# Second layer of a two-layer convolution kernel: three shared scale-and-result buffers, output stores on two queues, a split addition, shifted quantised rows

## The chip, the cores and the metric

The kernel runs on one core of a Trainium2 chip (trn2). The metric is the device time of one execution in microseconds. The profile is one further execution, recorded by the hardware profiler; its times count from the start of its span.

## The reference

The input x is 32 images of 8 channels, 256 x 256, float32. Two layers follow each other, each added to its own input:

```python
x = x + layer0(group_norm(x))     # a coupled map lattice of 15 steps, two small networks, a gate
x = x + layer1(group_norm(x))     # a quantised 3x3 convolution, 8 channels to 8
```

The change touches layer 1 alone. It quantises its normalised input with one scale for the whole batch, convolves whole numbers, scales back and adds a bias:

```python
def layer1(x, weight, bias):
    sx = 127 / max(abs(x));  sw = 127 / max(abs(weight))
    qx = clip(round(x * sx), -127, 127);  qw = clip(round(weight * sw), -127, 127)
    return conv3x3(qx, qw, padding=1) / (sx * sw) + bias
```

## The kernel before, in words

The first layer takes most of the time. Its program (lattice, hidden network, gate) works on groups of four images and leaves in a scratch tensor of device memory, `y_s[b]`, the sum x + layer0 of each image, with the image's mean, inverse deviation and largest deviation in small tiles. The maximum over the batch is needed before anything can be quantised, so the second layer starts only when the first is complete.

The second layer is the block `with ExitStack() as two` (from L879). An image is held as a tile of 128 partitions x 19 x 256 floats (`NB` = 19 bands, 2432 KB). A partition is one of 16 image rows of one of 8 channels; bands start 14 rows apart, so 14 of the 16 rows of a band are results and the outer two are the neighbours that a 3x3 convolution needs. Per image b, in the order of the source:

- the loads: three images ahead, one DMA of the whole tile `yb` (four buffers, pool `yp`). The first three are issued by SP, the others by ACT, after the activations of image b (L890, called at L936 to L937);
- L921: the scaling, three VectorE (DVE) instructions (first band, the 17 middle bands, last band) from `yb` into `tq`, the only buffer of its pool;
- L925: the rounding in place, by adding and taking away a large constant;
- L927: the clipping, written as bf16 into `qt`, one of two tiles taken in turn, whose rows are 258 wide: a zero at column 0, 256 values from column 1, a zero at column 257;
- L934: ten groups (two bands each, the last one band) of three TensorE (PE) matmuls, one for each horizontal shift dx, which read `qt` from column dx. Each group has one of four PSUM buffers `pt2`;
- L935: for each group a ScalarE (ACT) activation, which scales, adds the bias and writes two bands of `ob`, the result (two buffers, pool `op`);
- L938: one DVE addition of the whole tile, `ob` + `yb`;
- L941: 19 stores, one per band, each 14 rows of 8 channels (112 KB; the last band 4 rows, 32 KB), all issued by SP.

The order on each engine is the order of the source as the framework's scheduler moves it; it also puts in the waits. A buffer is given to its next user when all who read it are done, and a store is a reader of `ob`. Completion of a DMA is told by a semaphore; the program has eight of them for the DMAs of SP and ACT together and hands them out in turn, in the order in which it lists the DMAs. A DMA is issued only when the DMA that had its semaphore before has landed.

In the program as built the loads stand in pairs: the load of b+3 and that of b+4 lie one after the other on ACT's list, behind the activations of image b+1, and the second also waits for a buffer of `yb`. DVE's list takes the quantising of an image ahead of the addition of the image before.

Of the kernel before, what the change touches and what calls it, by code (L numbers as in the profile page):

```python
# [31 lines left out]
F32 = mybir.dt.float32  # L32
BF16 = mybir.dt.bfloat16
F32R = mybir.dt.float32r
AF = mybir.ActivationFunctionType
ALU = mybir.AluOpType
# [4 lines left out]
P = 128  # L41
C = 8
H = W = 256
# [3 lines left out]
MAX_Q = 127.0  # L47
ROUND = 1.5 * 2.0**23

NB = 19  # L50
STEP = 14
PW = W + 2
# [61 lines left out]
def kernel(  # L114
# [15 lines left out]
    nc = tc.nc  # L130
    B = x.shape[0]
    V, S, G, T = nc.vector, nc.scalar, nc.gpsimd, nc.tensor

    def dram_ap(t, offset, dims):
        return bass.AP(t.tensor, t.offset + offset, dims)
# [17 lines left out]
    qw = cp.tile([P, 3, P], BF16, name="qw")  # L153
# [103 lines left out]
    with ExitStack() as one:  # L257

        one.enter_context(tc.manual_schedule(engines={mybir.EngineType.PE}))
        pool = lambda name, bufs, **kw: one.enter_context(tc.tile_pool(name=name, bufs=bufs, **kw))  # L260
# [558 lines left out]
        def chain(*gens):  # L819
            for gen in gens:  # L820
                yield from gen
# [15 lines left out]
        def both(a, t_a, b, t_b):  # L837

            done_a = done_b = 0.0
            while a or b:  # L840
                if b is None or a and done_a * t_b <= done_b * t_a:
                    w = next(a, None)
                    if w is None:
                        a = None
                        continue
                    done_a += w
                else:
                    w = next(b, None)
                    if w is None:
                        b = None  # L850
                        continue
                    done_b += w
                yield w

        def prep(g, halves):
            return normalise([(b, half) for half in halves for b in range(g * GB, g * GB + GB)])

        def images(f, g):
            for b in range(g * GB, g * GB + GB):
                yield from f(b)  # L860
# [5 lines left out]
        for g in range(NG):  # L866
            fill, t = images(nca, g), T_NCA
            if g:
                fill, t = both(fill, t, images(gate, g - 1), T_GATE), t + T_GATE
            if g + 1 < NG:  # L870
                fill, t = both(fill, t, prep(g + 1, (0, 1)), T_PREP), t + T_PREP
            if g == 0:
                fill, t = chain(prep(0, (1,)), fill), t + 20.0
# [5 lines left out]
    with ExitStack() as two:  # L879


        pool = lambda name, bufs, **kw: two.enter_context(
            tc.tile_pool(name=name, bufs=bufs, reuse_waits="tile", **kw)
        )
        tp, qp, op, sp, yp = pool("tp", 1), pool("qp", 2), pool("op", 2), pool("sp", 1), pool("yp", 4)
        ps = pool("ps", 4, space=PSUM)

        def load(b):
            y = yp.tile([P, NB, W], F32, name="yb", tag="yb")
            (nc.sync if b < 3 else nc.scalar).dma_start(  # L890
                y, dram_ap(y_s[b], 0, [[W, P], [STEP * C * W, NB], [1, W]])
            )
            return y

        ys = {b: load(b) for b in range(3)}

        gmax = sp.tile([P, 1], F32, name="gmax")
        V.tensor_reduce(gmax, dev_y, AX.X, ALU.max)
        gall = sp.tile([P, 1], F32, name="gall")
        G.partition_all_reduce(gall, gmax, P, bass.bass_isa.ReduceOp.max)  # L900
        sx = sp.tile([P, 1], F32, name="sx")
        V.reciprocal(sx, gall)
        V.tensor_scalar(sx, sx, MAX_Q, None, ALU.mult)
        inv = sp.tile([P, 1], F32, name="inv")
        V.tensor_tensor(inv, sx, sw, ALU.mult)
        V.reciprocal(inv, inv)
        qs = sp.tile([P, 3, B], F32, name="qs")
        V.tensor_scalar(qs[:, 0, :], rstd_y, sx, None, ALU.mult)
        V.tensor_scalar(qs[:, 1, :], qs[:, 0, :], masks[:, 2:3], None, ALU.mult)
        V.tensor_scalar(qs[:, 2, :], qs[:, 0, :], masks[:, 3:4], None, ALU.mult)  # L910
        qt = [qp.tile([P, NB, PW], BF16, name=f"qt{i}", tag=f"qt{i}", bufs=1) for i in range(2)]
        for t in qt:
            V.memset(t[:, :, 0], 0.0)
            V.memset(t[:, :, PW - 1], 0.0)

        for b in range(B):
            y = ys.pop(b)

            t = tp.tile([P, NB, W], F32, name="tq", tag="tq")
            for k0, k1, i in ((0, 1, 1), (1, NB - 1, 0), (NB - 1, NB, 2)):  # L920
                V.tensor_scalar(  # L921
                    t[:, k0:k1, :], y[:, k0:k1, :], mean_y[:, b : b + 1], qs[:, i, b : b + 1],
                    ALU.subtract, ALU.mult,
                )
            V.tensor_scalar(t, t, ROUND, ROUND, ALU.add, ALU.subtract)  # L925
            q = qt[b % 2]
            V.tensor_scalar(q[:, :, 1 : 1 + W], t, MAX_Q, -MAX_Q, ALU.min, ALU.max)  # L927
            o = op.tile([P, NB, W], F32, name="ob", tag="ob")
            for p in range(10):
                k0, n = 2 * p, (2 if p < 9 else 1)  # L930
                pt = ps.tile([P, 512], F32, name="pt2", tag="pt2")
                pt = pt[:, : n * W].rearrange("p (k w) -> p k w", w=W)
                for dx in range(3):
                    T.matmul(pt, qw[:, dx, :], q[:, k0 : k0 + n, dx : dx + W], start=(dx == 0), stop=(dx == 2))  # L934
                S.activation(o[:, k0 : k0 + n, :], pt, AF.Identity, bias=bv[:, 3:4], scale=inv)  # L935
            if b + 3 < B:  # L936
                ys[b + 3] = load(b + 3)  # L937
            V.tensor_tensor(o, o, y, ALU.add)  # L938
            for k in range(NB):
                rows = STEP if k < NB - 1 else 4  # L940
                nc.sync.dma_start(  # L941
                    dram_ap(out, b * C * H * W + STEP * k * W, [[W, rows], [H * W, C], [1, W]]),
                    o[C : C + rows * C, k, :],
                )


# [43 lines left out]
```

## Time and profile before

| what | us |
|---|---|
| median of three runs | 14468.11 (14463.03 to 14472.73) |
| the profiled execution | 14447.83 |
| its span | 14446.0 |
| PE busy over the span | 13241.2 (92%) |
| DVE busy | 8161.7 (56%) |
| ACT busy | 4043.5 (28%) |
| POOL busy | 2458.8 (17%) |
| in the stretch 13680 to 14446: PE / DVE / ACT busy | 269.16 / 520.88 / 219.13 |
| in the same stretch: share of time the DMA engines are busy, mean rate | 0.61, 187 GB/s |

The page gives busy times for the whole program, and there the first layer dominates. The second layer is the last stretch: its first scaling starts at 13682.90 us and its last store is issued at 14442.98. Rows by line, waits and timelines can be asked for that stretch alone. In the views, a chain of waits lists the work that ended last, followed back from the end: at each step to what released it. "issue" is time in which nothing that the profile shows was waited for; SPq and ACTq are the issuing of DMAs by those engines; a row "DMA yb<-y_s" is the time from the issue of a load until it has landed.

### The profile page before, as it was taken

To read this page: it belongs to the slowest core of one execution; us is meant where nothing else is said; L and a number is where in the kernel's file an instruction comes from. 1 tells how busy PE (TensorE), PEld (TensorE's weight loads), DVE (VectorE), ACT (ScalarE), POOL (GpSimd) and SP (SyncE) were. 2 spreads that over 40 slices of the span, in tenths; PEclk is the share of its full clock that TensorE was granted. 3 is DMA by queue.
4 is the path that set the end of the run, shared out by engine and by line. 5 is a ranking of instruction groups with operands and counts; after the bars stand their busy time and mean duration, and the time that the engine had idled before them with its cause. 6 is when DMAs were issued, how large, how long until landed. Compare 5 with 4: busy or idle time off the path is not lost.

```text
span 14446.0 us, 229162 instructions
## 1 busy us (share of the span) xinstructions
PE 13241.2 (92%) x81728; PEld 6420.6 (44%) x81728; DVE 8161.7 (56%) x16290; ACT 4043.5 (28%) x6274; POOL 2458.8 (17%) x4266
## 2 busy tenths in 40 slices
PE   2999999999999999999999999999999999999733
PEld 1554444444444444444444444444444444444211
DVE  3555555555555555555555555555555555555576
ACT  1333223232322232222223222322232222222122
POOL 1110111111111111111111111111111111112300
PEclk9999999999999999999999999999999999999866
DMA  5444444444444444444344434444444433333365
GB/s 149 93 101 93 92 99 105 101 95 104 105 97 101 106 98 98 101 100 111 88 101 105 108 91 102 103 108 94 97 104 108 95 84 80 86 75 79 114 195 176
DMA packets 2259557, 1496.71 MB, mean 104 GB/s; under 512 B 1061248, under 2 KB 2229504, under 8 KB 2258304
## 3 DMA queue, kind: packets, MB, share of 16 engines
q1 hardware_dynamic: 2176976, 1401.95, 41.1%
q10 hardware_dynamic: 81456, 80.12, 1.7%
q8 instruction: 663, 10.86, 0.3%
q14 instruction: 462, 3.78, 0.1%
HBM read 866.48 MB, written 478.69 MB: 93 GB/s over the span
## 4 chain that ended last, share of the span: by engine, by line
PE 76%; DVE 7%; DMA 7%; SPq 4%; issue 3%; ACT 1%; POOL 1%; ACTq 1%; POOLq 0%; DVEq 0%
PE pt L486 34%; PE ph L563 19%; PE pa L755 13%; PE acc L580 7%; DVE gt L494 2%; PE pg L721 1%; DMA im<-xp_s 1%; DMA out_dram<-ob 1%; SPq L941 1%; PE pt L934 1%; DVE m_b L499 1%; DMA yb<-y_s 1%; DMA m_a<-m_a 1%; DMA xb<-in_x_dram 1%; DMA xr<-in_x_dram 1%
## 5 line engine op out<-in xcount | busy, mean ns | idle before, releaser
L486 PE MATMUL pt<-m_a,lw 128*64 128x390 f32 x17280 | 5857.6, 497 | 160.4 <-DMA m_a<-m_a 121.4
L486 PE MATMUL pt<-m_b,lw 128*64 128x384 f32 x17280 | 5825.7, 492 | 23.0 <-DVE m_b L410 17.8
L573 ACT ACTIVATE h<-ph,bp_sb 128x512 f32<-128x512 f32 x4096 | 2584.7, 685 | 6258.0 <-PE ph L563 6187.8
L486 PEld LDWEIGHTS pt<-m_a,lw 128*64 128x64 f32 x17280 | 2312.1, 138 | 1824.9 <-issue 1670.8
L486 PEld LDWEIGHTS pt<-m_b,lw 128*64 128x64 f32 x17280 | 2316.1, 138 | 1601.4 <-issue 1465.6
L563 PE MATMUL ph<-im,wp_hi 48*128 48x512 f32 x12288 | 2713.5, 416 | 104.8 <-DMA im<-xp_s 54.4
L494 DVE SCALAR_TENSOR_TENSOR gt<-pt,d_b 128x390 f32<-128x390 f32 x2880 | 1610.6, 559 | 1828.2 <-PE pt L486 1824.9
L494 DVE SCALAR_TENSOR_TENSOR gt<-pt,d_a 128x384 f32<-128x384 f32 x2880 | 1584.9, 550 | 1826.9 <-PE pt L486 1826.5
L563 PE MATMUL ph<-im,wp_lo 48*128 48x512 f32 x12288 | 2598.5, 399 | 0.0
L503 POOL TENSOR_TENSOR m_b<-m_b,junk 128x12 f32<-128x12 f32 x2688 | 809.2, 301 | 8089.7 <-DVE m_b L499 7597.8
L563 PEld LDWEIGHTS ph<-im,wp_hi 48*128 48x128 f32 x12288 | 1331.4, 188 | 1013.5 <-DVE m_b L499 197.8
L499 DVE SCALAR_TENSOR_TENSOR m_b<-gt 128x390 f32<-128x390 f32 x2688 | 1562.5, 581 | 42.5 <-DVE gt L494 0.9
L499 DVE SCALAR_TENSOR_TENSOR m_a<-gt 128x384 f32<-128x384 f32 x2688 | 1525.9, 568 | 15.6
L563 PEld LDWEIGHTS ph<-im,wp_lo 48*128 48x128 f32 x12288 | 1327.1, 188 | 215.2
L580 PE MATMUL acc<-h,wu_z 128*32 128x512 f32 x8320 | 1170.7, 605 | 12.9 <-ACT h L573 7.3
L755 PE MATMUL pa<-xnb,gw 128*64 128x512 f32 (+1 forms) x3840 | 890.5, 596 | 0.2
L755 PE MATMUL pa<-cmb,gw 128*64 128x512 f32 (+1 forms) x3840 | 852.0, 576 | 10.0 <-POOL cmb L677 10.0
L755 PE MATMUL pa<-nb,gw 128*64 128x512 f32 (+1 forms) x3840 | 849.5, 574 | 0.0
L726 POOL TENSOR_TENSOR d<-cmb,nb 128x512 f32<-128x512 f32 x320 | 511.4, 1598 | 1608.5 <-DVE gate L730 1449.6
L730 DVE TENSOR_TENSOR gate<-gate,d 128x512 f32<-128x512 f32 x320 | 216.0, 675 | 870.3 <-ACT gate L723 856.3
L934 PE MATMUL pt<-qt,qw 128*128 128x512 bf16 (+1 forms) x960 | 269.2, 451 | 477.9 <-ACT ob L935 427.1
L767 ACT ACTIVATE r<-pa,bv 128x512 f32<-128x512 f32 x320 | 213.1, 666 | 1651.3 <-PE pa L755 1650.3
(132 smaller groups left out, 6966.1 us busy)
## 6 DMA issues: line engine op xcount, KB each, us to landing
im<-xp_s SPq DMA_DIRECT2D x1152, 193.5 KB
im<-xp_s SPq DMA_DIRECT2D x1216, 96.8 KB
d_a<-xq_s SPq DMA_DIRECT2D x2048, 36.0 KB
nb<-nc_s SPq DMA_DIRECT2D x288, 256.0 KB
cq<-cm_s SPq DMA_DIRECT2D x288, 256.0 KB
yb<-y_s ACTq DMA_DIRECT2D x29, 2432.0 KB
xb<-in_x_dram SPq DMA_DIRECT2D x544, 128.0 KB
xp_s<-hi SPq DMA_DIRECT2D x256, 258.0 KB
```

The source lines that it names most:

```text
L486: T.matmul(pt[half], lw[:, c, k, half], beside if part == 2 else own, start=part < 2, stop=part > 0,)
L494: V.scalar_tensor_tensor(gt, pt, FLOOR, d[:, ts, :], ALU.max, ALU.add)
L499: V.scalar_tensor_tensor(to, gt, 1.0, gt, ALU.subtract, ALU.mult)
L503: G.tensor_tensor(edge, edge, junk.unsqueeze(1).to_broadcast([P, 6, 2]), ALU.mult)
L563: T.matmul(ph[:, :n].rearrange("p (h w) -> p h w", w=W), w[64 * i : 64 * i + 48, dx, :], rhs[:, :, dx : dx + W], start=(dx == 0 and w is w ...
L573: S.activation(h[:, :n], ph[:, :n], AF.Relu, bias=bp_sb)
L580: T.matmul(acc[32 * g : 32 * g + 32, :cols], wu_z[:, 24 - 8 * i : 56 - 8 * i], h, start=first, stop=last,)
L726: G.tensor_tensor(three(d), cmb[:, :n, 1 : 1 + W], nin, ALU.subtract)
L730: V.tensor_tensor(y[:, :cols], gt[:, :cols], d[:, :cols], ALU.mult)
L755: T.matmul(three[half], gw[:, s * 3 + dx, half], t[:, :n, dx : dx + W], start=(i == 0), stop=(i == 8),)
L767: S.activation(r1[:, : n * W], pa[:, : n * W], AF.Relu, bias=bv[:, 0:1])
L934: T.matmul(pt, qw[:, dx, :], q[:, k0 : k0 + n, dx : dx + W], start=(dx == 0), stop=(dx == 2))
```

## The change

The scaled input and the result now share a buffer: `t` and `o` are one tile of the pool `op`, which has three buffers in place of two, and the pool `tp` is gone. An activation writes over values that the clipping has read. The rows of `qt` are 260 wide, with two zeros on each side and the 256 values from column 2; the matmuls read from columns 1, 2 and 3. The addition is made in two instructions, bands 0 to 9 and bands 10 to 18. The stores of bands 0 to 9 are issued by SP after the addition; those of bands 10 to 18 are issued by ACT one image later, after the next image's activations and the next load, and the last image's after the loop.

```diff
-        tp, qp, op, sp, yp = pool("tp", 1), pool("qp", 2), pool("op", 2), pool("sp", 1), pool("yp", 4)
+        qp, op, sp, yp = pool("qp", 1), pool("op", 3), pool("sp", 1), pool("yp", 4)
...
-        qt = [qp.tile([P, NB, PW], BF16, name=f"qt{i}", tag=f"qt{i}", bufs=1) for i in range(2)]
+        qt = [qp.tile([P, NB, W + 4], BF16, name=f"qt{i}", tag=f"qt{i}") for i in range(2)]
         for t in qt:
-            V.memset(t[:, :, 0], 0.0)
-            V.memset(t[:, :, PW - 1], 0.0)
+            V.memset(t[:, :, 0:2], 0.0)
+            V.memset(t[:, :, W + 2 : W + 4], 0.0)
+
+        def store(queue, b, o, ks):
+            for k in ks:
+                rows = STEP if k < NB - 1 else 4
+                queue.dma_start(
+                    dram_ap(out, b * C * H * W + STEP * k * W, [[W, rows], [H * W, C], [1, W]]),
+                    o[C : C + rows * C, k, :],
+                )
+
+        waiting = None
         for b in range(B):
             y = ys.pop(b)
-            t = tp.tile([P, NB, W], F32, name="tq", tag="tq")
+            t = op.tile([P, NB, W], F32, name="ob", tag="ob")
...
-            V.tensor_scalar(q[:, :, 1 : 1 + W], t, MAX_Q, -MAX_Q, ALU.min, ALU.max)
-            o = op.tile([P, NB, W], F32, name="ob", tag="ob")
+            V.tensor_scalar(q[:, :, 2 : 2 + W], t, MAX_Q, -MAX_Q, ALU.min, ALU.max)
+            o = t
...
-                    T.matmul(pt, qw[:, dx, :], q[:, k0 : k0 + n, dx : dx + W], start=(dx == 0), stop=(dx == 2))
+                    T.matmul(pt, qw[:, dx, :], q[:, k0 : k0 + n, dx + 1 : dx + 1 + W], start=(dx == 0), stop=(dx == 2))
                 S.activation(o[:, k0 : k0 + n, :], pt, AF.Identity, bias=bv[:, 3:4], scale=inv)
             if b + 3 < B:
                 ys[b + 3] = load(b + 3)
-            V.tensor_tensor(o, o, y, ALU.add)
-            for k in range(NB):
-                rows = STEP if k < NB - 1 else 4
-                nc.sync.dma_start(
-                    dram_ap(out, b * C * H * W + STEP * k * W, [[W, rows], [H * W, C], [1, W]]),
-                    o[C : C + rows * C, k, :],
-                )
+            if waiting:
+                store(nc.scalar, *waiting)
+            for ks in (slice(0, 10), slice(10, NB)):
+                V.tensor_tensor(o[:, ks, :], o[:, ks, :], y[:, ks, :], ALU.add)
+            store(nc.sync, b, o, range(0, 10))
+            waiting = (b, o, range(10, NB))
+        store(nc.scalar, *waiting)
```

In the changed program as built, from image 3 on, each image has the same list. ACT: ten activations of image b, the load of b+3, nine stores of b-1. SP: ten stores of b. DVE: the first two scalings of b+1, the two additions of b, the last scaling, the rounding and the clipping of b+1. The scaling of b+1 waits for all stores of b-2, whose buffer it writes.

## The prediction

> **What bounds the kernel now.** I looked first at the page's slices: TensorE is full until the last three of 40, so only the end, the second layer (from about 13682 us of the span to 14446.0), can be touched by this change. There I read the waits by engine, then SP's own waits, then the chain that ended last, then the timeline of one pair of images.
>
> Waits in that stretch (engine and line, what ended the wait, us in total, times, longest):
> ```profile
> ACT ob L935 <- DMA out_dram<-ob: 455.0, 29, 26.4
> PE pt L934 <- ACT ob L935: 427.1, 30, 25.6
> DVE qt L927 <- PE pt L934: 121.8, 12, 10.6
> ...
> SPq L941 <- DMA yb<-y_s: 129.4, 28, 12.3
> ```
> ACT waits for stores that free the result buffer, PE for ACT, DVE for PE. The last line says where the stores are late: 28 times, once for each load after the first ones, SP holds a store back until a *load* has landed. The reason is in the program: eight DMA semaphores are handed out in turn, and a DMA is not issued before the one that held its semaphore eight places earlier has landed, on whichever queue that was.
>
> The chain, one pair of images (start, us, what):
> ```profile
> 13713.48 12.49 DMA yb<-y_s
> ...
> 13761.01 9.55 DMA yb<-y_s
> ...
> 13893.10 2.12 DMA out_dram<-ob
> ...
> 13901.89 10.68 DMA yb<-y_s
> ...
> 13912.58 0.82 SPq L941
> ...
> 13949.61 10.55 DMA yb<-y_s
> ```
> A load is issued at 13901.89 and lands after 10.68; SP is released at 13912.58 and issues, 0.87 us apart (0.82 and the gap), 31 more stores of this and the next image; the last lands 2.12 after its issue, ACT starts, and the next pair's first load goes out at 13949.61. A pair takes 47.72, an image **23.86**. The sum closes: 10.7 (load) + 31 x 0.87 (27.0) + a second, shorter hold of SP and hand-overs (1.4) + 2.1 + 6.5 (ACT until the load) = 47.7. So the queue of stores is the largest term, the load's landing the second. The compute engines have room:
> ```profile
> L927 DVE TENSOR_SCALAR qt<-tq 128x4864 bf16<-128x4864 f32 x32 | 167.1, 5222 | 123.8 <-PE pt L934 121.8 <-DVE tq L925 0.5
> L938 DVE TENSOR_TENSOR ob<-ob,yb 128x4864 f32<-128x4864 f32 x32 | 167.1, 5221 | 95.6 <-ACT ob L935 66.6 <-DMA out_dram<-ob 29.0
> L925 DVE TENSOR_SCALAR tq<-tq 128x4864 f32<-128x4864 f32 x32 | 86.2, 2694 | 1.1
> ```
> With the scaling's 3.19, DVE needs 16.3 of 23.86 per image.
>
> **The change, part by part.**
>
> *Shared buffer, three deep.* No instruction goes. The scaling of image b+2 now waits for the stores of b-1; before, only the activations and additions waited for stores. DVE's queue behind that wait holds the addition of b+1, so the wait can delay stores.
>
> *Addition in two parts.* 5.22 becomes 2.82 + 2.56 (slope between L938 and the 512-wide addition at L730, 0.69 us: 1.04 ns an element): DVE +0.16, but the first store may go 2.4 earlier.
>
> *Quantised rows at an even place.* The question is L927's 5.22 against L925's 2.69 for the same count.
> ```profile
> L342 DVE CAST hi<-xr x128: 679/693/698, 127.5 to 11497.8; 128x1024 fp32r<-128x1024 f32 x128
> ```
> L342 also writes padded rows from column 1, four rows of 256, and is no slower (693 ns) than the dense L331 (810 ns). An odd place alone is no brake there, though its elements have four bytes. Bounds: 2.69 and 5.22; I take 5.22, its own row. DVE has room between images, so the other end is worth only what lies bare: about five quantisations at the head and the tail, 5 x 2.5 = 12 us off the end.
> [...]
>
> *Stores on two queues.* SP issues 10 per image, ACT the other 9 one image late, behind the next load and ahead of the next activations. The new order of DMAs is: load of b+3 (ACT), ten stores of b (SP), nine of b-1 (ACT). With eight semaphores in turn this gives a lockstep: SP's eighth store waits for the load's landing; ACT's first eight wait for the landing of SP's third to tenth; ACT's activations of b+1 queue behind all nine; the next load queues behind those. It is a loop, once per image:
> 1. Load, issue to landing: 9.55 with no store beside it, 10.68 with three, 12.49 with about ten. SP has seven beside it here, issued from 0.3 before it to 4.9 after: **11.5**.
> 2. SP's eighth, ninth and tenth: two spacings 1.74, then landing. The trace's landing events put a 112 KB store at 2.43 from its issue when no load is beside it. ACT's stores, held behind the load on their ring, move just then, so I add 0.15: **4.3**.
> 3. ACT's eighth store 0.87 and its short ninth 0.66 (SP's prices): **1.5**. The trace has no such store on ACT; its load issues cost 0.37, so the two lie between 0.7 and 1.7.
> 4. Ten activations until the next load may be issued: in the timeline of the pair, 13928.54 to 13936.39 and 13895.48 to 13902.82, 7.85 and 7.34: **7.6**.
> 5. Six hand-overs of 0.05: **0.3**.
>
> Sum 25.2 per image against 23.86. Five store issues are left on the loop where it had 15.5 per image, but each image now pays a whole load landing and ten activations; before, a pair shared these. DVE fits: after the load's issue it needs 2.56 + 0.41 + 2.69 + 5.22 = 10.9 to quantise the next image, and ACT is free for it only at 17.5. Hence both DVE edits are hidden, and so is the quantisation's own write.
>
> *Head and tail, from the same rows.* Images 0 to 3: the same DVE work until 13705.3, first stores at 13708.2 (13713.4 before); the load of image 4 at 13714.5 lands 12.3 later and holds SP, then ACT, to 13732.6; then scaling, rounding and quantising of image 3 stand ahead of the addition of 2 (14 us), and one more lockstep follows: the load of image 6 goes out at 13762.5 (13761.0 before). From there 25 periods to the last load, 14392.5, and one less 0.3 to image 29's first store: 14417.4. The tail has no loads but ACT's queue is now long: nine stores of 28 ahead of the quantisation of 30 (10.2 with landing), 5.7 for it, 10.8 for image 31's, 10.5 until its last activations (9.6 as for image 0, and one store among them), then 17 stores at 0.87 and the last landing (16.0): 53.2. End at **14470.6**, against 14445.1 for the last landing before: **+26**, 0.18%.
>
> The profiled execution took 14447.83, its span 14446.0; the median of the runs is 14468.11, 20 above it, from outside what I change. I add 26 to the median: **14494**.
>
> **The rivals.**
>
> *A. Two queues get in each other's way* (slower; 0.20). Landings beside other traffic are 2.9 to 3.6 in the trace where a lone one is 2.43, and stores beside a load 6 to 7. If the landing in step 2 is 3.3 (the step 5.0), the load 12.1 and ACT's issues 1.7, the period is 26.7, 1.5 x 26 more: +65, 14533. For it: ACT's first stores are released by the load just when SP's eighth goes. Against: the DMA engines are busy 0.61 of the stretch, by its row of stages. It decides from a period of 25.5 up, where the change is slower by more than 0.2%.
>
> *B. The shorter store queue wins* (faster; 0.12). If the load does not hold SP, what is left is nine spacings and a landing, 10.3, ACT's last two stores, 1.5, activations, 7.6, hand-overs, 0.3: 19.7 per image, 26 x 5.5 = 143 less than the forecast: -117, 14351. For it: stores are 27.0 of the pair's 47.7, and ACT's 455 us are all stores. Against: the 28 holds by loads, each of which the new order keeps. It decides from a period below 23.0.
>
> *C. The place matters after all* (0.10): quantisation 2.69, loop unchanged, +14: 14482, no change that can be told.
>
> **How the numbers follow.** The forecast has 0.58. Its own spread is the load at 10.8 to 12.1 and 0.3 either way for the other steps: period 24.2 to 26.1, 0 to +49. For the range I keep it and A, and go below it for the cheap issue on ACT (-0.8 per image) with a load near its short end: 14440 to 14535. Left out are B and extremes that need every term at one end (a load at 9.55 with 6.83 for the activations gives 21.6; a load at 12.49 with 8.35 and 3.6 gives 28).
> A measurement of this kernel tells about 0.2% from no change, 29 us. Slower by more: A, and 0.45 of the forecast's 0.58: 0.46. Faster by more: B and a remnant: 0.13. Between: 0.41.
>
> **What would show it.** Right: SP's store line waits once per image for a load, seven stores before and three after it; the activations start some 0.7 after ACT's last store; loads 25.2 apart; the scaling's first piece waits for stores; L927's successor at 5.2. Wrong: loads under 23 apart (B), a store on ACT costing ACT several us, stores landing late with no load beside them (A), or DVE busy without a gap, which would put the quantisation on the loop.

## The result and the profile after

The first measurement gave 14480.51 us for the changed kernel (median of 4 runs, 14471.66 to 14491.7) against 14466.45 for the kernel before (4 runs): a ratio of 1.001, with a 95% interval of 0.9992 to 1.0027. A second one on another chip, with 11 runs against 21, gave 14427.99 against 14427.19: **1.0001**, 0.9992 to 1.0010. So no difference can be told. The forecast of +26 us is a ratio of 1.0018: inside the first interval, above the second. The change costs less than forecast, and what is left of it is too small to see.

The profiled execution took 14478.06, its span 14476.3. That is 30 us more than before, and the first thing to ask is where. The first load of the second layer is issued at 13695.20; before it was 13667.39. So 27.8 of the 30 lie in the first layer, which the change doesn't touch. From that load to the last landing the second layer takes 780.1 us, against 777.7 before: +2.4.

Waits of the changed kernel from 13690 to the end (engine and line, what ended the wait, us in total, times, longest); the last two are those of SP's queue:
```profile
ACT ob L945 <- DMA out_dram<-ob: 465.7, 27, 19.9
...
PE pt L944 <- DVE qt L937: 387.0, 32, 23.1
DVE ob L931 <- DMA out_dram<-ob: 217.7, 29, 9.2
```
```profile
SPq L920 <- DVE ob L951: 317.9, 29, 17.8
SPq L920 <- DMA yb<-y_s: 107.7, 27, 6.1
```
ACT still waits for stores, about as long as before (455.0), though now only because its own nine stores stand in its queue ahead of the activations. The scaling (L931) waits 29 times for stores: the shared buffer's new wait. SP is held by a load once per image, 27 times at 4.0 us each.

The chain that ended last, one image of it (start, us, what):
```profile
13987.79 11.64 DMA yb<-y_s
...
13999.45 0.81 SPq L920
...
14000.37 2.62 DMA out_dram<-ob
...
14003.06 0.82 ACTq L920
...
14004.84 0.68 ACTq L920
...
14005.62 0.79 ACT ob L945
...
14006.44 2.73 PE pt L944 x6
...
14011.63 11.79 DMA yb<-y_s
```
It is the loop of the prediction, step by step: a load lands, SP is released, its ninth and tenth store follow, the tenth's landing lets ACT's last stores out, the activations start 0.78 us after the issue of the last of them begins, and the next load goes out. The chain takes this way in 16 of the 25 periods between the loads of images 6 and 31; in the other 9 it takes another, which the next section shows. The loop lasts 23.84 here; over the loads of images 6 to 31 the mean is **24.22**, where 25.2 was forecast and the kernel before has 23.45.

Groups of the second layer (busy us, mean ns, idle before and what ended it):
```profile
L951 DVE TENSOR_TENSOR ob<-ob,yb 128x2560 f32<-128x2560 f32 x64 | 170.0, 2685 | 3.2 <-ACT ob L945 2.9
L937 DVE TENSOR_SCALAR qt<-ob 128x4864 bf16<-128x4864 f32 x32 | 167.0, 5220 | 3.5 <-DVE ob L935 0.5
```
The clip at its even place takes 5220 ns, before 5222. The addition in two parts costs 170.0 - 167.1 = 2.9 us of DVE's busy time in all.

### The profile page after: what moved, and what is told of

It is laid out like the page before. It is cut to its first block, busy times and chain, and to the rows that moved or that the text cites. A ratio compares the mean times of both kernels' runs of the same rounds, so it can differ in the third digit from the quotient of the medians.

```text
span 14476.3 us, 229083 instructions
## 1 busy us (share of the span) xinstructions
PE 13280.4 (92%) x81728; PEld 6439.6 (44%) x81728; DVE 8166.0 (56%) x16322; ACT 4037.1 (28%) x6274; POOL 2450.3 (17%) x4266
## 5 line engine op out<-in xcount | busy, mean ns | idle before, releaser
L563 PE MATMUL ph<-im,wp_hi 48*128 48x512 f32 x12288 | 2721.1, 417 | 111.2 <-DMA im<-xp_s 53.2
L944 PE MATMUL pt<-qt,qw 128*128 128x512 bf16 (+1 forms) x960 | 301.8, 485 | 454.1 <-DVE qt L937 387.0
```

Source lines behind the costliest of these rows:

```text
L563: T.matmul(ph[:, :n].rearrange("p (h w) -> p h w", w=W), w[64 * i : 64 * i + 48, dx, :], rhs[:, :, dx : dx + W], start=(dx == 0 and w is w ...
L944: T.matmul(pt, qw[:, dx, :], q[:, k0 : k0 + n, dx + 1 : dx + 1 + W], start=(dx == 0), stop=(dx == 2))
```

## The experiments

The theory: the loop of five steps sets the time ("theory 1"). Its main rivals: the throughput of the DMA engines sets it ("theory 2"); DVE with its slow clip sets it ("theory 3"). All kernels but the two of "before" are the changed kernel or edits of it. "Second layer" is always the time from its first load's issue to the last landing in the one profiled execution; the ratio is that of the timed runs to the kernel before on the same chip.

| kernel | first layer until | second layer | us per image, loads 6 to 31 | ratio, 95% interval |
|---|---|---|---|---|
| before | 13667.4 | 777.7 | 23.45 | 1 |
| before, again | 13660.0 | 774.6 | 23.38 | |
| changed | 13695.2 | 780.1 | 24.22 | 1.001, 0.9992 to 1.0027 |
| changed, again | 13642.5 | 767.2 | 23.74 | 1.0001, 0.9992 to 1.0010 |
| load behind ACT's stores | 13633.5 | 729.5 | 22.62 | 0.9968, 0.9955 to 0.9980 |
| loads on GpSimd | 13653.4 | 749.0 | irregular | 0.9985, 0.9976 to 0.9995 |
| stores on one queue | 13646.6 | 743.9 | 22.40 | 0.9981, 0.9972 to 0.9990 |
| clip in 18 rows + 1 | 13644.2 | 766.8 | 24.31 | 0.9999, 0.9989 to 1.0008 |
| before, clip in 18 rows + 1 | 13646.1 | 762.2 | 23.15 | |
| 18 rows, eight PSUM buffers | 13663.6 | 683.4 | 21.33 | 0.9938, 0.9924 to 0.9953 |
| nine stores, one for a channel | 13643.7 | 775.7 | 23.84 | 0.9999, 0.9990 to 1.0008 |
| load behind, 18 rows | 13645.5 | 657.7 | 20.22 | 0.9915, 0.9901 to 0.9928 |
| the same, four shared buffers | 13648.4 | 637.8 | 19.47 | 0.9911, 0.9894 to 0.9927 |
| the same, eight PSUM buffers too | 13654.2 | 615.5 | 18.82 | 0.9891, 0.9876 to 0.9906 |

### Both kernels again: is the first layer changed?

No edit.

> The kernel before once more, on the chip that also runs the changed kernel once more, for the two stretches of each. If the first layer's program is the same to the chip in both kernels, the 27.8 us by which the changed kernel's first layer ended later in the first two profiles is spread between executions, and here the two first layers end within some 15 us of one another, in either order. If the change moves the first layer (code or buffers placed elsewhere), the changed kernel's first layer ends later again by more than that. The second layer takes 777 to 780 us again.

> The changed kernel once more, with more rounds. By the loop of five steps the second layer takes 780 us again, 1 to 4 us longer than before's; the ratio of the times is then 1.000 to 1.0005 if the first layers are alike, and 1.001 to 1.002 if the changed kernel's first layer is later as a rule.

The changed kernel's first layer ended 17.5 us *earlier* this time. No edit of the table touches the first layer, and still the second starts at times that differ by 17.5 to 27.8 us between the profiles of one chip, and by 62 over all of them (13633.5 to 13695.2). The 27.8 us lie within such spread, and nothing shows them to be a price of the change. The expectation of a ratio of 1.000 to 1.0005 held. That of the second layer didn't: 767.2, not 780, and 7 us less than before's 774.6 instead of 1 to 4 more. The chain of this profile shows what differs. Only 7 of the 25 periods go through a load. The other 18 go through a second loop (start, us, what):
```profile
13966.14 2.14 DMA out_dram<-ob
...
13968.73 2.54 DVE ob L931
13971.27 2.74 DVE ob L951
...
13975.83 6.37 DMA out_dram<-ob
...
13982.27 0.82 ACTq L920
...
13989.38 2.14 DMA out_dram<-ob
```
The scaling waits for the landing of ACT's last store, because it writes over that store's buffer; the first addition stands behind it on DVE; SP's stores follow, and the third of them, beside the load, lands in 6.37; only then may ACT issue its nine stores, the last of which the next scaling waits for. From one addition to the next this takes 23.4. So the shared buffer's wait and the divided addition are on the path in 18 of 25 periods here and in 9 of 25 in the first profile, while the rounding and the clip are not. Which of the two loops a period takes goes with the pace of TensorE, as the part on eight PSUM buffers shows; the images are called fast or slow by that pace.

### The load behind ACT's stores

```diff
-            if b + 3 < B:
-                ys[b + 3] = load(b + 3)
             if waiting:
                 store(nc.scalar, *waiting)
+            if b + 3 < B:
+                ys[b + 3] = load(b + 3)
```

> The load of image b+3 is issued behind ACT's nine stores of b-1 instead of ahead of them; all else as in the changed kernel. Theory 1 (lockstep: the period is the load's landing, three stores, ACT's last stores and its activations in a row, 24.22 us per image): the load's semaphore is now met again only four SP stores into the next image, so its landing runs beside the ten activations (7.8) and the addition (2.8) and holds nothing. The loop is activations 7.8 + first addition 2.8 + nine store spacings 7.8 + a landing and ACT's last store 1.5 to 3 + the load's issue 0.4, some 20.5 to 21.5 per image; 26 images: the second layer 70 to 100 us shorter than 780. Theory 2 (the DMA engines' throughput sets the period): the same bytes, so 24.2 per image and 780 again. Theory 3 (DVE, with the quantisation's 5.22, sets it): no change either.

The second layer is 38 to 51 us shorter than in the two runs of the changed kernel, and the timed runs agree: 0.9968. Moving one load is worth more than all four edits of the change, with the same bytes, so theory 2 falls. But the period is 22.62, not 20.5 to 21.5. The chain says why:
```profile
13995.16 2.83 DVE ob L951
13998.00 0.81 SPq L920
...
13998.86 2.42 DMA out_dram<-ob
14001.30 0.82 ACTq L920
...
14003.99 2.22 DMA out_dram<-ob
...
14006.29 3.20 DVE ob L931 x3
14009.52 2.70 DVE ob L935
...
14012.32 3.70 DVE qt L937
```
No load is on it any more. The loop now runs from the addition through SP's second store, whose landing frees a semaphore for ACT's last four stores of the image before, to the scaling, which waits for these because it writes over their buffer, and on through rounding and clip to the next addition: 2.8 + 0.9 + 2.4 + 2.7 + 2.3 + 3.2 + 2.7 + 5.2 = 22.2. What the prediction called hidden, the shared buffer's wait and the clip, is the path as soon as the load is off it.

### The loads on GpSimd

```diff
-            (nc.sync if b < 3 else nc.scalar).dma_start(
+            (nc.sync if b < 3 else nc.gpsimd).dma_start(
```

> The loads from image 3 on are issued by GpSimd, whose DMAs have semaphores of their own, so no store waits for a load's landing; all else as in the changed kernel. Theory 1 (lockstep): step 1 of the loop, 11.6 us of load, leaves it. What is left is stores (nine to ten spacings and a landing, 10 to 11), ACT's last stores 1.5 to 2.3, and activations 7.8: 19.5 to 21 per image, the second layer 85 to 120 us shorter than 780. Theory 2 (throughput of the DMA engines): 24.2 per image, no change. Theory 3 (DVE): no change.

The ratio is 0.9985 and the second layer 18 to 31 us shorter: a gain, as theory 1 wants, but a quarter of it. No store waits for a load's semaphore, yet the chain shows what took the hold's place:
```profile
14019.25 9.40 DMA out_dram<-ob
...
14028.72 0.82 ACTq L920
```
That is a *store*, issued 2.5 us after a load, that needs 9.40 to land, where a lone one takes 2.4. ACT's next store waits for it. Freed of the load's semaphore, the queues are held by the slow landings of the stores beside the load.

### All nineteen stores on SP

```diff
-            if waiting:
-                store(nc.scalar, *waiting)
...
-            store(nc.sync, b, o, range(0, 10))
-            waiting = (b, o, range(10, NB))
-        store(nc.scalar, *waiting)
+            store(nc.sync, b, o, range(0, NB))
```

> All nineteen stores of an image go out on SP directly behind its addition, none on ACT; the shared buffers, the addition in two parts and the even place stay. It shows what the second queue alone did. Theory 1 (lockstep through the shared semaphores): ACT no longer queues behind stores, so a load goes out while SP still issues the image before, and SP is held for at most 11.6 less seven spacings of 0.87, 5.5 per load. The period is 19 x 0.87 = 16.5 plus 1 to 5.5: 17.5 to 22, so the second layer is 60 to 170 us shorter than with two queues: the second queue was the loss and the third buffer the gain. Rival (two queues are worth their parallel issue): 31 spacings, a load and a landing per pair again, 24 to 28 per image, 0 to 100 longer. Theory 2 (throughput): 24.2, no change.

743.9: shorter than with two queues (767.2, 780.1) and than before (774.6, 777.7). So the second queue, with the delay of its nine stores by one image, takes back what the rest of the change gives: 31 to 34 us gained without it, 23 to 36 lost with it. The direction is that of theory 1, the size less than the 60 expected, as the period is 22.4 and not 17.5 to 22. Stores beside a load are slow here too (7.7 us), and DVE, which waits 179.0 us for the shared buffer's stores, has its part in the path. Which of the buffer and the divided addition brings the 30 us wasn't separated.

### The clip in 18 rows and one, at both places

In the changed kernel, and with columns 1 to 256 in the same way in the kernel before:
```diff
-            V.tensor_scalar(q[:, :, 2 : 2 + W], t, MAX_Q, -MAX_Q, ALU.min, ALU.max)
+            for k0, k1 in ((0, NB - 1), (NB - 1, NB)):
+                V.tensor_scalar(q[:, k0:k1, 2 : 2 + W], t[:, k0:k1, :], MAX_Q, -MAX_Q, ALU.min, ALU.max)
```

> The clip at the even place is cut into one instruction of 18 rows and one of a single row; all else as in the changed kernel. The reading that the odd count of 19 rows, not the place, keeps the clip at 5.22: 18 rows take 2.5 to 2.7 and the single row 0.2 to 0.4. The rival, that the clip is slow for its padded rows or its bf16 result: 4.9 to 5.0 and 0.3 to 0.4. For the time, theory 1 (lockstep): DVE is not on the loop, so the period stays 24.2 and only the head and the tail get shorter: the second layer 5 to 12 us shorter. Theory 3 (DVE on the loop): 2.3 per image, 60 to 75 us shorter.

> The kernel before with the clip cut into 18 rows and one, at its odd place. If the count of rows decides and the place does not, the 18 rows take the same 2.5 to 2.7 here at the odd place as they took at the even one (2.58 with the single row 0.27 apart from it); if the place counts too, they take 4.9 to 5.0. For the time, as DVE waits for others in this kernel: the second layer 774 to 778 us as before, less at most 12 at the head and the tail.

The clip's group in the changed kernel (even place), then in the kernel before (odd place):
```profile
L938 DVE TENSOR_SCALAR qt<-ob 128x4608 bf16<-128x4608 f32 x32 | 81.9, 2560 | 3.5 <-DVE ob L935 0.5
```
```profile
L928 DVE TENSOR_SCALAR qt<-tq 128x4608 bf16<-128x4608 f32 x32 | 82.0, 2563 | 129.9 <-PE pt L935 128.2
```
18 rows (4608 elements) take 2560 ns at the even place and 2563 at the odd one, 19 rows (4864) 5220 and 5222. So the 18 rows take half the time of the 19 at either place, and the place makes 2 to 3 ns. Which property of the 19 rows does it was not shown: only 19 and 18 were run. The edit of the place was the right operation and the wrong property.

For the time, the kernel before gains 12 to 15 us in its second layer, where at most 12 were expected. The changed kernel gains nothing that can be told: 766.8 against 767.2 and 780.1 in the two profiles of the changed kernel (each on another chip), 0.9999 against 1.0001 to the kernel before on the same chip. Its head and tail did get 14.6 shorter (766.8 less 25 x 24.31 against 767.2 less 25 x 23.74), but against that run the loop got slower by 25 x 0.57 = 14.3. Beside the first run (24.22) the loop is hardly slower. 21 of its 25 periods go through a load, and all its images are slow ones, as the next part shows.

### Eight PSUM buffers: the pace of TensorE

Two images of the changed kernel, one of the first and one of the second profiled execution (start, us, engine, line; x = instructions; in brackets the idle time before):
```profile
14005.62 6.49 ACT L945 ACTIVATE ob<-pt,bv,inv 128x512 f32<-128x512 f32 x9 [16.89 <-DMA out_dram<-ob]
14006.44 5.14 PE L944 MATMUL pt<-qt,qw 128*128 128x512 bf16 x18 [2.53 <-ACT ob L945]
...
14011.63 0.37 ACTq L890 DMA_DIRECT2D yb<-y_s  x1
```
```profile
13966.91 5.46 ACT L945 ACTIVATE ob<-pt,bv,inv 128x512 f32<-128x512 f32 x8 [16.73 <-DMA out_dram<-ob]
13967.73 3.83 PE L944 MATMUL pt<-qt,qw 128*128 128x512 bf16 x18 [0.66 <-ACT ob L945]
...
13971.61 0.37 ACTq L890 DMA_DIRECT2D yb<-y_s  x1
```
TensorE fills four PSUM buffers ahead and then waits for ACT, 2.53 us in the one image, 0.66 in the other. The next 18 matmuls take 5.14 and 3.83, and the load goes out 6.01 and 4.70 after the first activation. What it waits for is the end of TensorE's work: in each image from 4 to 28 of both runs the load's issue starts 0.31 to 0.32 us after the start of the image's last matmul. The pace differs from image to image, and in every image from 4 to 29 of both runs the pause tells which it is: where the starts of the 12th and 13th matmul are 1.3 to 2.3 us apart (24 images), the ten activations start within 5.98 us; where they are 2.45 or more apart (28 images), within 6.3 to 7.8. In the first image above the first matmuls after the pause come 0.43 us apart, in the second 0.217. A shorter clip lets TensorE's four groups begin sooner, so the pause grows: in the kernel with 18 rows it is 4.3 to 6.0 in every image, and no image has the fast pace.

The profile's granted clock goes with the pace. Stretches of the two images, one behind the other (us; busy us of PE, PEld, DVE, ACT and POOL; granted clock, share of the DMA engines' time, GB/s):
```profile
13999.09:14002.50 3.41, 2.65 (x7) 1.01 (x8) 0.70 (x1) 0.00 (x0) 0.00 (x0) 0.50 0.66 204
14002.50:14005.91 3.41, 1.41 (x7) 0.53 (x6) 0.00 (x0) 0.29 (x1) 0.00 (x0) 1.00 0.57 170
14005.91:14009.33 3.42, 2.89 (x7) 1.01 (x7) 2.05 (x2) 3.28 (x6) 0.00 (x0) 0.50 0.04 11
```
```profile
13964.02:13967.43 3.41, 3.05 (x8) 0.92 (x7) 0.00 (x0) 0.53 (x1) 0.00 (x0) 0.50 0.47 135
13967.43:13970.84 3.41, 3.11 (x14) 1.34 (x14) 2.44 (x2) 3.41 (x6) 0.00 (x0) 1.00 0.03 10
```
In the first image TensorE is busy for 1.41 of the 3.41 us from 14002.50, which hold the pause; in the next stretch the clock is 0.5, and the matmuls come 0.43 us apart. In the second image it is busy for 3.05 of the 3.41 us from 13964.02; in the next stretch the clock is 1.0, from 0.30 us ahead of the matmuls behind the pause, and they come 0.217 apart. So the two paces are those at a granted clock of 0.5 and of 1.0. Why the longer pause goes with the lower clock was not shown: no run changed the pause alone.

The pace goes with the loop. In both runs all 24 periods that begin with the load behind a fast image take the second loop, and 23 of the 26 behind a slow image take the load's.

```diff
-        ps = pool("ps", 4, space=PSUM)
+        ps = pool("ps", 8, space=PSUM)
```

> The changed kernel with the clip in 18 rows and one (second layer 766.8 us, period 24.3) and eight PSUM buffers instead of four for the result, so that TensorE runs eight of ten groups ahead and not four. Theory 4: the fourth term of the loop, the activations, is long where TensorE paused over 2.4 us between its fourth and fifth group and then takes 0.43 us a matmul: 6.3 to 7.5 us from first to last activation, against 5.97 where the pause was shorter and a matmul took 0.217. With eight groups ahead ACT no longer waits for TensorE: 5.97 or less each time, the load issued 4.7 behind the first activation and landing in 10.4 to 10.8. Period 23.2 to 23.7, the second layer 15 to 28 us shorter than 766.8. Rival: the pace of TensorE is without weight (what differs is the traffic of the stores): 24.2 to 24.4 again.

(The rest is the kernel with 18 rows.) 683.4: shorter by 83, where 15 to 28 were expected. The ten activations start within 5.97 in each image, as expected. But the load goes out 2.94 us after the first of them on average, not 4.7, and it lands in 9.50 after its issue (11.80 in the kernel with 18 rows), being further ahead of SP's stores. With that the load is off the path: in the chain none of the 25 periods goes through one, and all take the second loop. One image shows the issue:
```profile
13997.95 4.79 ACT L946 ACTIVATE ob<-pt,bv,inv 128x512 f32<-128x512 f32 x7 [13.69 <-DMA out_dram<-ob]
...
14002.43 0.36 ACTq L890 DMA_DIRECT2D yb<-y_s  x1
14002.60 1.93 ACT L946 ACTIVATE ob<-pt,bv,inv 128x512 f32<-128x512 f32 x3
```
Three activations that stand ahead of the load in ACT's program start after its issue; in 13 of the 25 images from 4 to 28 six do. So it isn't the activations that hold the load back but the last of them that has to wait for TensorE. Pace and wait both went with this edit; how the 83 us divide between them wasn't separated.

### Load behind, 18 rows, more buffers

The load's edit and the clip's edit together; then also a fourth shared buffer; then also eight PSUM buffers:
```diff
-        qp, op, sp, yp = pool("qp", 1), pool("op", 3), pool("sp", 1), pool("yp", 4)
+        qp, op, sp, yp = pool("qp", 1), pool("op", 4), pool("sp", 1), pool("yp", 4)
```

> The load behind ACT's stores, as in the kernel of 729.6 us, and the clip in 18 rows and one. Theory 1b: once the load's landing is off the loop, the loop runs through DVE: scaling (which waits for the stores of the shared buffer) 3.2, rounding 2.7, clip 5.2, the first addition 2.8, the first store, and back over ACT's last stores. The clip is then on it, and its 2.3 us come off the period: 22.6 to 20.3 us, the second layer 50 to 65 us shorter than 729.6. Rival: that period too is set by the stores and activations alone, with DVE beside them; then the cut is worth 13 us, as with the load in its first place.

> The kernel of 657.7 us (load behind ACT's stores, 18 rows) with a fourth buffer for scaled input and result, so that the scaling waits for the stores of an image earlier. Theory 1b (its loop runs through the wait of the scaling for the shared buffer's stores, then scaling 3.2, rounding 2.7, clip 2.8, addition 2.8): that wait goes, and with it the loop. Next is the loop of the stores: some 4 us of activations, the first addition 2.8, nineteen stores on two queues 9 to 10.5, the load's issue 0.5 and a hand-over: 17 to 19 us per image against 20.2, the second layer 30 to 80 us shorter than 657.7. Rival (the stores alone set it, and DVE only waits beside them): no change.

> Load behind ACT's stores, clip in 18 rows and one, four shared buffers, eight PSUM buffers: what the experiments point to, together. If the loop is the one of the stores (activations until the addition may start, addition, nineteen stores on two queues, the load's issue), TensorE's pace costs it some 1 to 2 us per image and the eight buffers take that away: 16 to 18 us per image, a second layer of 540 to 620 us, and 1.1 to 1.6% less time than before. If DVE is the bound by then, 14.3 of work per image is the floor.

With the load out of the way the clip is on the path: 22.62 to 20.22 per image, 72 us shorter in the second layer, a little more than expected, and its own edit that was worth nothing before is now worth 0.5% of the kernel. Stretches of 200 us (busy us of each engine; behind them the granted clock, the share of the DMA engines' time and GB/s), of the changed kernel and of the one with 18 rows and the load behind:
```profile
13900.00:14100.00 200.00, 79.02 (x251) 29.75 (x252) 134.36 (x57) 53.84 (x80) 0.00 (x0) 0.69 0.61 195
```
```profile
13900.00:14100.00 200.00, 96.19 (x299) 35.29 (x298) 137.49 (x79) 65.78 (x100) 0.00 (x0) 0.72 0.72 228
```
The DMA share rises from 0.61 to 0.72: there was room, and theory 2 is done with. The fourth shared buffer brings 20 us in the profile, less than the 30 expected, and nothing that the timed runs can tell (0.9911 after 0.9915). In the last kernel's chain, over one and a half images, 69.0% is the landing of stores, 7 us each beside a load:
```profile
14011.30 6.98 DMA out_dram<-ob
...
14025.68 7.07 DMA out_dram<-ob
```
Its period is 18.82, above the 16 to 18 expected, and its 14266.15 us against 14427.53 are the least of all: **0.9891**.

### Nine larger stores

```diff
+            for c in range(C):
+                queue.dma_start(
+                    dram_ap(out, (b * C + c) * H * W, [[W, STEP], [STEP * W, NB - 1], [1, W]]),
+                    o[C + c : C + c + STEP * C : C, 0 : NB - 1, :],
+                )
...
+            store(nc.sync, b, o)
```

> The same bytes of each image go out in nine stores on SP, one for each channel over 18 bands (258 KB each) and the short one, instead of nineteen on two queues; all behind the second part of the addition; all else as in the changed kernel. Theory 1: the number of stores sets the loop, by issues of 0.87 and by the semaphores that they hand on; with nine, SP needs 7.8 us, one load's landing is met once per image at the seventh store, and DVE's 16.6 per image is next: 17 to 20.5 us per image, the second layer 95 to 190 us shorter than 780. Theory 2 (the DMA engines' throughput for these bytes sets the period): 24 again, no change. Rival: stores with only 14 source partitions each take longer than twice as long, and the holds on landings grow: slower than 780.

Half the stores, and 23.84 per image: no change. But it isn't theory 2, as the timeline shows:
```profile
13999.80 3.19 DVE L933 TENSOR_SCALAR ob<-yb,mean_y,qs 128x256 f32<-128x256 f32 x3
...
14005.82 5.22 DVE L939 TENSOR_SCALAR qt<-ob 128x4864 bf16<-128x4864 f32 x1
14011.10 9.07 PE L946 MATMUL pt<-qt,qw 128*128 128x512 bf16 x30 [14.82 <-DVE qt L939]
...
14018.09 2.83 DVE L951 TENSOR_TENSOR ob<-ob,yb 128x2560 f32<-128x2560 f32 x1 [7.05 <-ACT ob L947]
...
14023.69 3.19 DVE L933 TENSOR_SCALAR ob<-yb,mean_y,qs 128x256 f32<-128x256 f32 x3
```
Scaling to scaling is 23.89 us, and no DMA stands in between. The scheduler has put DVE's instructions into another order: the addition of an image now comes ahead of the next image's quantisation, not behind it, so one image's quantisation, matmuls, five activations and addition follow one another without overlap, with TensorE's first four groups at its slow pace (1.28 us each). The stores are off the path, and another loop of about the same length stands behind them. Its last 18 periods are 23.89 each; why they come so near the changed kernel's 24.22 and 23.74 was not shown.

## Why the prediction was right, and where it was off

- **The time** lies in the range, but that says little: the range of 95 us also holds the kernel before. What speaks for the mechanism is the chain, and it does so in part.
- **The loop** is there with its five steps and its order, but it is the path in 16 of 25 periods of the first run and in 7 of the second. Over all periods, from load to load: step 1, the load, 11.5: measured 11.56 (10.99 in the second run). Step 2, SP's last three stores and a landing, 4.3: 4.49 (4.37); its 0.15 supposes that ACT's stores are held behind the load, and in each of the first run's images 7 to 31 ACT's first store, issued up to 3.60 us before the load's landing, lands 0.3 to 2.9 behind it. Step 3, ACT's last two, 1.5: 2.26 (3.04); undisturbed it is 1.6 to 1.7, but when the load is early, ACT's stores and not SP's come last, and up to 4.5 go here; that is the second loop. Step 5, 0.3: 0.12 up to the first activation.
- **Step 4 was mis-sized**: ten activations until the next load, 7.6, measured 5.80 (5.22). It was read off two rows of the kernel before, from the first activation to the end of the last. But the load of the same pair goes out 6.41 after the first (13895.48 to 13901.89), and the prediction's own closing sum has 6.5 there: that is 1.2 of the 1.8. The rest is the pace: in the kernel before TensorE pauses 6 to 26 us ahead of its fifth group and goes on at its slow pace (0.43 a matmul); in the changed kernel the pause is 1.3 to 4.5, and either pace follows. The prediction took the interval to be ACT's work. It is a wait for TensorE, and the load isn't held by the activations as such (with eight PSUM buffers: 2.94). The sum comes to 24.2 (23.7) instead of 25.2: 25 x 0.98 = 24.5, less 1.5 that the head took more, is the 23 us by which the second layer stayed below the 803 of the forecast.
- **Head and tail**: the load of image 6 was to go out 1.5 us later than before, counted from the first load; it was 3.0. From image 29's first store to the end 53.2 was forecast and 53.0 measured.
- **The place** gained nothing, as forecast (the clip at 5.22, measured 5.220); rival C falls. **The divided addition and the shared buffer** were costed at nothing because the lockstep hides them. That holds where a load leads, in 16 and 7 of 25 periods. In the others both are on the path, the wait and the first addition, and with the load moved they are on it throughout.
- **Rival B** (the shorter queue wins if no load holds SP) did not come about in the changed kernel, but its condition was right and its price too good: with the load moved the period is 22.6 and not 19.7, because DVE is next. **Rival A** (queues in each other's way) stayed below its point, a period of 25.5: SP's tenth store lands in 2.4 to 2.9 in the first run, but for two images (3.4 and 3.6), and in 2.4 to 2.8 in the second, but for one (3.3). The landing of a store beside a load, 6.2 to 6.8, is on the path, though: as a step of the second loop.
- **The head start of 20 us** between profile and median was carried over from the kernel before. The first layer's own spread, 17.5 to 27.8 us between profiles of one chip, is what limits any statement on a change of this size from one execution.

What stays open: how much of the one-queue kernel's 30 us belongs to the third buffer and how much to the divided addition; and what decides which pace an image gets (17 of 26 are fast in the second run, 7 in the first).

## What to carry to other kernels

A queue that is relieved only helps if it was the loop, so write down the loop before and after, with each wait that a DMA inherits from the one eight places earlier, and look for a second loop of nearly the same length; moving one load gained 0.3% where the second queue gained nothing. Where a large load must go out, put it where the next DMAs that share its semaphores are not urgent. And a term read off one kernel is worth checking for what it waits on: the stretch from the first activation to the load was 6.4, 5.8 or 2.9 us, depending on how far TensorE had run ahead and at which clock.

## What the runs showed of the hardware

- In the images shown of the changed kernel a matmul of 512 columns comes every 0.43 us at a granted clock of 0.5 and every 0.217 at 1.0.
- With eight PSUM buffers, ACT's load was issued while up to six activations ahead of it in its program had not started (13 of 25 images), so its place in the program isn't when it goes out.
- A store of 112 rows of 1 KB landed in 2.43 us alone, in 6 to 8 when issued early beside a load on the other queue, and in 9.4 and 10.1 in a chain beside loads that GpSimd issued.
- A store of 252 such rows, from 14 partitions 8 apart, landed in 3.5 to 5.3 us (all but nine of 256) and cost SP 0.81 to 1.38 (once 2.55).
- With 19 rows the clip took 5.22 us, with 18 it took 2.56; its even or odd place made 2 to 3 ns.
